# Normalisation units and output projections of an attention layer, kept in two lists instead of one

## The chip, the cores and the metric

The kernel runs on one core of a Trainium2 chip. The metric is the device time of one execution in microseconds, the median of several runs. The profile shows one further execution, with the start and the duration of every instruction on TensorE (PE, and PEld for its weight loads), VectorE (DVE), ScalarE (ACT), GpSimd (POOL) and on SyncE's DMA queue (SP).

## The reference

Four graph layers run one after the other on 2708 nodes with 128 features. Each layer takes a layer norm and a relu of x and adds its result to x. The second is an attention layer, and the change lies there:

```python
def _L1_gnn_ref(x, spatial_encoding, edge_encoding, Wq, Wk, Wv, Wo):
    n, d = x.shape
    h = Wq.shape[0] // d                  # 8
    scale = d ** (-0.5)
    q = (x @ Wq.T).reshape(d, n, h)       # 128 "heads" of 8 columns
    k = (x @ Wk.T).reshape(d, n, h)
    v = (x @ Wv.T).reshape(d, n, h)
    a = jnp.einsum('dnh,dmh->dnm', q, k) * scale
    a = a + spatial_encoding + edge_encoding     # adj, twice
    a = jax.nn.softmax(a, axis=2)
    out = jnp.einsum('dnm,dmh->dnh', a, v)
    out = out.reshape(n, h * d)
    return out @ Wo.T
```

The reshape of `out` matters for the order of the work: a row of the matrix that meets Wo is 1024 neighbouring numbers of the buffer [128 heads, 2708 nodes, 8]. So 128 rows of the output projection need some six heads complete, with all their nodes, and not a slice of every head. Layer 2 (a graph layer that multiplies by the adjacency matrix) needs the layer norm of the rows that come out.

## The kernel before, in words

The 2708 rows lie in 22 tiles of 128 (the last has 20). The 128 heads are worked in 64 pairs (`d`), and two pairs make one of NG = 32 groups of GRP = 4 heads.

*The attention loop.* The softmax over all nodes is taken from a polynomial: moments of keys and values over all nodes, evaluated for every query. The loop runs over the 64 pairs and, in each, over NCH = 6 chunks `c` of the row tiles. One such step issues transposes of the query features (`turn`, L1524, copied out by ACT at L1528), matmuls with the moments (`evaluate`, L1538), a product and a reduction on DVE (L1546, L1555), and parts of the preparation of the next two pairs: query features on DVE and key features on POOL (both by the helper line L802/L805), and the moments (`moments`, L869, weighed on DVE at L883). Every group's sums go to DRAM as `o_g` (`sums`, L1091).

*The work beside the loop.* A step counter `n` counts the 384 steps. A chain of generators, `first`, is advanced by some yields a step; it sorts the nodes, and it computes the exact terms of each node's neighbours, which land in DRAM as `more_n`. When it is exhausted, four calls of `step` follow every step of the loop. `step` advances a generator that is due, or, where none is, lets `begin` start a new one. There are two kinds:

- `normalise(u)`, a unit u. It loads the sums of its heads (L1382 or L1384) and the neighbour terms (L1385), waits LOAD steps, adds them on POOL (L1395), then SOON (one step) later forms the reciprocal (L1400) and the quotients (L1405) on DVE, and then stores the heads to `o_d` with three DMAs (`store_heads`, L551). Units 0 to 14 hold two groups (eight heads), and their sums and terms take two tiles `r_o` and `r_c` of the ring `big` (5 tiles). Units 15 and 16 hold one group, in one tile `r_both`. The last one waits for the end of the loop (HOLD).
- `projected(t)`, a row tile t, by `project_out`. It loads 128 rows of `o_d` (L1034), waits LOAD steps, transposes them with eight matmuls (L1043), lets ACT copy them (L1049), multiplies by Wo (L1061), adds to x on DVE (L1065) and forms the statistics for the layer norm (`measured`, L999). It takes both tiles of one of the rings `c_v` and `c_q`, so that at most two projections are under way. Only one of them may be in its transposes (`turning`) and one in its matmuls (`adding`).

*The order.* Before, one list `beside` holds both kinds in a fixed order, and `begin` only looks at its head. A projection that needs unit `need` stands in it behind unit need + 1, and begins when no unit up to `need` is under way any more, that is, one step after the store was issued. DMAs are issued by SP in their program order: a load that has to wait for the store that it reads holds up those behind it. The two last row tiles (`final`) need the last unit and are projected within layer 2 (L1798).

*After the loop.* Whatever is left of `beside` runs with no attention work between its steps (`while beside or under_way`). Layer norms of groups of four row tiles follow (`normed2`: L1005, L1007, L1008, L1012, and the transposes `turned2`, L1025 and L1026); in the loop they run as soon as four tiles are known. In the last pair, the first four rows of the adjacency matrix for layer 2 are fetched (`rows_of_adj2`, L993), into buffers of the key and query features as these come free. Then comes a branch on `flag`, and the matmuls of layer 2 (L1846).

Of the kernel before, what the change touches and what calls it, by code (L numbers as in the profile page):

```python
# [20 lines left out]
GRP = 4  # L21
# [25 lines left out]
def gnn4_kernel(  # L47
# [28 lines left out]
    NG = C // GRP  # L76
# [129 lines left out]
    with ExitStack() as ph:  # L206
# [56 lines left out]
        with tc.manual_schedule():  # L263
# [37 lines left out]
            for t in begun_with:  # L301
                i = order.index(t)
# [39 lines left out]
            last = iter(())  # L342
            for t0, tw in _cuts(NT, 4):
# [4 lines left out]
                last = now  # L348
# [197 lines left out]
    def store_heads(eng, h0, src):  # L546

        flat = o_d[h0 * N : (h0 + src.shape[1]) * N].rearrange("(i n) k -> i n k", n=N)
        even = WHOLE // 16 * 16
        for p0, p1, nt in ((0, even, NT), (even, WHOLE, NT), (WHOLE, WHOLE + 1, LEFT)):  # L550
            eng.dma_start(  # L551
                flat[:, p0 * NT : p0 * NT + (p1 - p0) * nt].rearrange(
                    "i (p t) k -> p i (t k)", t=nt
                ),
                src[p0:p1, :, :nt].rearrange("p i t k -> p i (t k)"),
            )
# [369 lines left out]
    with ExitStack() as ph:  # L926
# [10 lines left out]
        with tc.manual_schedule():  # L937
# [9 lines left out]
            n = 0  # L947
# [70 lines left out]
    def turned2(t0, t1, pt, copy):  # L1018

        s0 = rows[t0][0]  # L1020
        w = rows[t1 - 1][0] + rows[t1 - 1][1] - s0
        for t in range(t0, t1):
            sz = rows[t][1]
            o = (t - t0) * P
            nc.tensor.transpose(pt[:, o : o + sz], h2[:sz, t], ident[:sz, :sz])  # L1025
        copy(hT2[:, s0 : s0 + w], pt[:, :w])  # L1026
# [41 lines left out]
        measured(t)  # L1068
        known.append(t)

    LOAD, SOON = 4, 1

    with ExitStack() as ph:
        lp = ph.enter_context(tc.tile_pool(name="l1_c", bufs=1, reuse_waits="tile"))
        big = ph.enter_context(tc.tile_pool(name="l1_big", bufs=5, reuse_waits="tile"))
# [283 lines left out]
            yield  # L1361

        def unit_of(g):
            return g // 2 if g < NG - 2 else g - NG // 2 + 1

        NU = unit_of(NG - 1) + 1

        def normalise(u):

            last, two = u == NU - 1, u < NU - 2  # L1370
            nh = GRP * (1 + two)
            h0 = nh * u if two else (NG - NU + u) * GRP
            g = h0 // GRP
            if two:
                ro, co = (
                    big.tile([P, NT * nh * VW], FP, name=f"r_{e}", tag="big") for e in "oc"
                )
            else:
                both = big.tile([P, 2, NT * nh * VW], FP, name="r_both", tag="big")
                ro, co = both[:, 0], both[:, 1]  # L1380
            if two:
                nc.sync.dma_start(ro, o_g[u].rearrange("p j x -> p (j x)"))  # L1382
            elif not last:
                nc.sync.dma_start(ro, o_g[g // 2][:, g % 2])  # L1384
            nc.sync.dma_start(  # L1385
                co.rearrange("p (t x) -> p t x", t=NT),
                more_n[:, h0 : h0 + nh].rearrange("(p t) i k -> p t (i k)", t=NT),
            )
            yield LOAD
            if last:  # L1390
                yield HOLD
            js = 1 + two
            out_ = ro.rearrange("p (j t x) -> p j t x", j=js, t=NT)
            own = ros.pop(g).rearrange("p t i k -> p t (i k)")[:, None] if last else out_
            nc.gpsimd.tensor_tensor(  # L1395
                out_, own, co.rearrange("p (t j x) -> p j t x", j=js, t=NT), ALU.add
            )
            yield SOON
            rs = sm.tile([P, NT * GRP * 2], FP, name="r_rs")[:, : NT * nh]
            nc.vector.reciprocal(rs, ro.rearrange("p (a k) -> p a k", k=VW)[:, :, HEAD])  # L1400
            on = co[:, : nh * NT * HEAD].rearrange("p (i t k) -> p i t k", i=nh, t=NT)
            sums_of = ro.rearrange("p (j t i k) -> p j t i k", j=js, t=NT, k=VW)
            inv = rs.rearrange("p (j t i) -> p j t i", j=js, t=NT)
            for j in range(js):
                nc.vector.tensor_tensor(  # L1405
                    on[:, j * GRP : (j + 1) * GRP].rearrange("p i t k -> p t i k"),
                    sums_of[:, j, :, :, :HEAD],
                    inv[:, j, :, :, None].to_broadcast([P, NT, GRP, HEAD]),
                    ALU.mult,
                )  # L1410
            yield SOON
            store_heads(nc.sync, h0, on)
            yield SOON

        pace = [1.75]

        def faster():

            pace[0] = 4.0
            yield  # L1420

        first = chain(by_node(), sorted_rows(), faster(), from_neighbours())
        beside = []
        done = 0
        late, final = [], []
        for t, (r0, sz) in enumerate(rows):
            need = unit_of(min((((r0 + sz) * P - 1) // N) // GRP, NG - 1))
            while done <= need:
                beside.append((done, done, True))
                done += 1  # L1430
                while late and late[0][1] <= done - 2:
                    beside.append(late.pop(0))
            if need < NU - 1:
                late.append((t, need, False))
            else:
                final.append(t)
        beside += late
        groups = [(t, min(t + 4, final[0])) for t in range(0, final[0], 4)]
        to_turn, norms = [], []
        in_turn = [t for t in range(NT) if t not in final]  # L1440
# [12 lines left out]
        under_way = []  # L1453
        rings = {"big": [], "c_v": [], "c_q": []}
        room = {"big": 5, "c_v": 2, "c_q": 2}
# [8 lines left out]
        def projected(t, ring):  # L1464

            nat, oT = (tm.tile([P, HD], FP, name="o_nat", tag=ring) for _ in range(2))
            both = nat, oT.rearrange("p (k c) -> p k c", k=KC)
            yield from project_out(both, turn_bank, sum_bank, woT, t)

        def begin(summed):  # L1470

            if not beside:
                return None
            i, need, norm = beside[0]
            last = norm and i == NU - 1
            if need >= summed and not last:
                return None
            if not norm and any(e[2] <= need for e in under_way):
                return None
            takes = 1 if norm and i >= NU - 2 else 2  # L1480
            for ring in ("big",) if norm else ("c_v", "c_q"):
                if sum(e[4] for e in rings[ring]) + takes <= room[ring]:
                    beside.pop(0)
                    gen = normalise(i) if norm else projected(i, ring)
                    entry = [gen, None, need if norm else NU, True, takes]
                    rings[ring].append(entry)
                    under_way.append(entry)
                    return entry
            return None

        def step(n, summed):


            entry = next((e for e in under_way if e[1] <= n), None)
            if entry is None:
                entry = begin(summed)
            if entry is None:
                return False
            wait = next(entry[0], None)
            if wait is None:  # L1500
                entry[3] = False
                under_way.remove(entry)
                for ring in rings.values():
                    while ring and not ring[0][3]:
                        ring.pop(0)
            else:
                entry[1] = n + wait
            return True
# [105 lines left out]
        with tc.manual_schedule():  # L1614
            soon, wanted = [], []
            n, owed = 0, 0
# [5 lines left out]
            for d in range(D):  # L1622
                asked, keyed = {}, {}
                for c in range(NCH):
# [36 lines left out]
                    if first is None:  # L1661
                        owed = 0
                        for _ in range(4):
                            step(n, unit_of(max((d - 1) // PG, 0)))
                        if d < D - 1:
                            normalising()
# [4 lines left out]
                g = d // PG  # L1671
# [12 lines left out]
            copies_by = [nc.vector.tensor_copy, nc.scalar.copy]  # L1684
            for e in under_way:
                e[1] = min(e[1], n)
            while beside or under_way:
                if to_turn:
                    turned2(*to_turn.pop(0), ps_g.tile([P, BK], FP, name="g_ps"), copies_by[0])
                    copies_by.reverse()  # L1690
                if not step(n, NU):
                    n += 1
# [8 lines left out]
    with ExitStack() as ph:  # L1701
# [127 lines left out]
        with tc.tile_pool(name="l2_pa", bufs=1, space=PSUM) as pa, tc.manual_schedule():  # L1829
            pgs = [pa.tile([C, BK], FP, name=f"pg{c}") for c in range(NC)]  # L1830
            beside = last_rows()
# [169 lines left out]
    with ExitStack() as ph, tc.manual_schedule():  # L2001
# [15 lines left out]
        def weighed(t):  # L2017
            sz, k = rows[t][1], ROOM[t]
            g = gs[t]
            z = gating(zp, g[:, 1 : k + 1], g[:, 0, C:], sz, k)  # L2020
            yield
            zs[t] = weighing(zp, g[:, 1 : k + 1], z, sz, l_val[:, t, :k], k)
            yield
# [29 lines left out]
        for t in range(NT + 4):  # L2053
# [3 lines left out]
            two = weighed(t - 1) if 0 <= t - 1 < NT else iter(())  # L2057
# [5 lines left out]
    with tc.tile_pool(name="l3_more", bufs=2) as mp, tc.tile_pool(  # L2063
# [3 lines left out]
        last = m1.tile([P, NT], FP, name="last")  # L2067
# [4 lines left out]
        with tc.For_i(0, nc.values_load(ovf, min_val=0, max_val=1)):  # L2072
# [24 lines left out]
            with tc.For_i(0, rounds):  # L2097
                for t, (r0, sz) in enumerate(rows):
# [35 lines left out]
                    g = mp.tile([P, 8, 2 * C], FP, name="g")  # L2134
# [3 lines left out]
                    e = mp.tile([P, C], FP, name="extra")  # L2138
# [48 lines left out]
```

## Time and profile before

| | |
|---|---|
| median of 3 runs | 2151.55 us (2151.46 to 2160.33) |
| the profiled execution | 2157.09 us, its span 2155.3 us |
| mean granted TensorE clock | 0.894 |
| PE busy | 1692.6 us, 79% of the span |
| DVE busy | 1444.2 us, 67% |
| POOL busy | 1321.0 us, 61% |
| ACT busy | 931.8 us, 43% |
| L1395, a unit of eight heads on POOL | 15 times, 3562 ns |
| L1400, its reciprocal on DVE | 15 times, 1246 ns |
| L1405, its quotients on DVE | 30 times, median 916 ns, at most 3191 ns |
| units of four heads | L1395 twice, 1859 and 1856 ns; L1400 twice, 680 ns; L1405 twice, 891 ns |

A row of the profile names the start or the number of instructions, the engine, the line, the operation and the tiles (out<-in). In a timeline the first number is the start from the beginning of the span and the second is the busy time in us; in brackets stands how long the engine had been idle, and what it had been waiting for. A row of waits reads: who waited, for whom, us in all, how often, the longest. A row of windows gives for each stretch its length, then the busy us of each engine with the number of instructions, the granted clock, the DMA share and GB/s.

### The profile page before, as it was taken

The page shows a single profiled execution, that of the slowest core. Times are in us where ns is not written, and L with a number is a line of the kernel's source. Part 1 is how long each engine was busy: PE and PEld are TensorE (multiplying, and loading weights), DVE is VectorE, ACT ScalarE, POOL GpSimd, SP SyncE. Part 2 cuts the span into 40 slices and gives each one's busy share as a digit, 9 for nine tenths or more (in the row PEclk, how much of TensorE's full clock was granted, in tenths as well). Part 3 has the DMA queues.
Part 4 walks back from the last instruction along what each step waited for, and adds up shares of the span by engine and source line. Part 5 has one row for each costly group of instructions (what it writes and reads, how often), then busy time and mean ns, then how long its engine had stood idle before and what let it go on. Part 6 is the DMA issues. An engine that isn't in the chain of part 4 may idle for free. (4 is left out here: it accounts for less than half of the span.)

```text
span 2155.3 us, 30079 instructions
## 1 busy us (share of the span) xinstructions
PE 1692.6 (79%) x10634; PEld 1348.4 (63%) x10634; DVE 1444.2 (67%) x3232; ACT 931.8 (43%) x2049; POOL 1321.0 (61%) x1363
## 2 busy tenths in 40 slices
PE   4767989988889788988888888888889769943442
PEld 3656864488789666666666665667889745423431
DVE  6899846366677788888888888877788720134331
ACT  3947744376677444444444444444445210021010
POOL 1343332066566699999999999997667210057762
PEclk9978999999999999999999999988999979965555
DMA  4755319778799676667766766764767757433331
GB/s 158 298 164 191 134 57 363 294 246 249 240 300 318 177 245 239 225 238 255 252 231 240 237 244 245 250 237 143 228 202 223 242 152 276 155 138 104 94 100 38
DMA packets 256854, 453.68 MB, mean 210 GB/s; under 512 B 112267, under 2 KB 180110, under 8 KB 231483
## 3 DMA queue, kind: packets, MB, share of 16 engines
q1 hardware_dynamic: 225459, 282.79, 39.6%
q0 software_dynamic: 31232, 168.86, 23.0%
q8 instruction: 85, 1.39, 0.3%
q14 instruction: 78, 0.64, 0.1%
HBM read 336.99 MB, written 114.60 MB: 210 GB/s over the span
## 5 line engine op out<-in xcount | busy, mean ns | idle before, releaser
L1538 PE MATMUL g_ps<-mw,fT 128*124 128x124 f32 x2816 | 377.9, 277 | 10.8 <-DVE mw L883 6.2
L869 PE MATMUL m_ps<-y,fk 123*128 123x128 f32 (+1 forms) x2816 | 372.6, 278 | 0.2 <-POOL fk L805 0.2
L1538 PEld LDWEIGHTS g_ps<-mw,fT 128*124 128x124 f32 x2816 | 344.5, 192 | 12.0 <-DVE mw L883 7.1
L869 PEld LDWEIGHTS m_ps<-y,fk 123*128 123x128 f32 (+1 forms) x2816 | 345.6, 194 | 1.3 <-issue 1.0
L1528 ACT COPY fT<-f_ps 128x496 f32<-128x496 f32 (+1 forms) x384 | 208.6, 543 | 242.1 <-PE f_ps L1524 239.9
L1291 PE MATMUL v_ps<-c_v,ident 128*128 128x512 f32 (+1 forms) x484 | 254.3, 651 | 74.7 <-DVE c_v L1274 74.0
L805 POOL TENSOR_TENSOR fk<-kv_t 128x264 f32<-128x264 f32 (+3 forms) x256 | 188.5, 761 | 186.4 <-ACT kv_t L833 185.6
L1546 DVE TENSOR_TENSOR z<-g_ps,bq 124x360 f32<-124x360 f32 (+1 forms) x384 | 191.1, 498 | 163.3 <-PE g_ps L1538 151.0
L1524 PE MATMUL f_ps<-ident,fq 124*128 124x124 f32 x1408 | 222.9, 278 | 94.1 <-DVE fq L802 63.8
L1250 POOL TENSOR_TENSOR c_kv<-c_kv,c_q 128x1024 f32<-128x1024 f32 (+1 forms) x121 | 284.3, 2350 | 5.0 <-DMA c_kv<-kv_n,srt 3.4
L1524 PEld LDWEIGHTS f_ps<-ident,fq 124*128 124x128 f32 x1408 | 167.4, 145 | 188.5 <-issue 90.1
L805 POOL TENSOR_TENSOR y<-kv_t 128x704 f32<-128x704 f32 x128 | 191.0, 1492 | 67.6 <-PE m_ps L869 67.0
L1555 DVE TENSOR_REDUCE o_raw<-z 124x72 f32<-124x360 f32 (+1 forms) x384 | 190.7, 497 | 13.2
L1291 PEld LDWEIGHTS v_ps<-c_v,ident 128*128 128x128 f32 (+1 forms) x484 | 86.8, 200 | 151.7 <-DVE c_v L1274 69.2
L1256 DVE TENSOR_REDUCE c_c<-c_kv 128x128 f32<-128x1024 f32 (+1 forms) x121 | 148.0, 1223 | 50.2 <-POOL c_kv L1250 47.7
L1263 ACT ACTIVATE c_c<-c_c 128x128 f32<-128x128 f32 (+1 forms) x121 | 31.7, 262 | 330.6 <-DVE c_c L1256 312.9
L805 POOL TENSOR_TENSOR fk<-fk,kv_t 128x440 f32<-128x440 f32 (+2 forms) x192 | 154.9, 821 | 5.5 <-ACT fk L772 5.3
L1274 DVE TENSOR_TENSOR c_v<-c_kv,c_c 128x1024 f32<-128x1024 f32 (+1 forms) x121 | 146.6, 1211 | 0.0
L1235 POOL DMA_INDIRECT c_kv<-kv_n,srt x121 | 118.0, 975 | 22.3 <-issue 8.6
L1974 POOL DMA_INDIRECT g<-tab_d,l_nbr x99 | 103.5, 1045 | 30.2 <-issue 29.8
L957 PE MATMUL qkv_ps<-wT,hT 128*128 128x512 f32 (+1 forms) x264 | 116.9, 601 | 0.4 <-ACT hT L438 0.4
L170 POOL TENSOR_TENSOR n_hot<-n_hot,n_fl 128x640 f32<-128x640 f32 (+1 forms) x22 | 34.0, 1545 | 119.6 <-DVE n_hot L164 116.0
(315 smaller groups left out, 2989.0 us busy)
## 6 DMA issues: line engine op xcount, KB each, us to landing
a_nat<-in_adj_dram SPq DMA_DIRECT2D x34, 1354.0 KB
raw<-qkv_d SPq DMA_DIRECT2D x128, 275.0 KB
qkv_d<-qkv SPq DMA_DIRECT2D x21, 1600.0 KB
n_raw<-qkv_d SPq DMA_DIRECT2D x96, 275.0 KB
kv_n<-n_kv SPq DMA_DIRECT2D x16, 1408.0 KB
fk<-in_adj_dram SPq DMA_DIRECT2D x12, 1354.0 KB
o_g<-o_raw SPq DMA_DIRECT2D x31, 396.0 KB
fq<-in_adj_dram SPq DMA_DIRECT2D x9, 1354.0 KB
```

Source lines behind the costliest of these rows:

```text
L805: nc.gpsimd.tensor_tensor(o, x, y, ALU.mult)
L869: nc.tensor.matmul(pms[d][:, :P], fks[d][:sz, t].rearrange("p i f -> p (i f)"), wide[h][:sz, o : o + P], start=t == 0, stop=t == NT - 1,)
L1235: nc.gpsimd.indirect_dma_start(out=kvs[b][:sz, e].rearrange("p c e k -> p (c e k)"), out_offset=None, in_=kv_n.rearrange("n c k -> n (c k) ...
L1250: nc.gpsimd.tensor_tensor(k, k, qs[t][:sz], ALU.mult)
L1256: nc.vector.reduce_sum(cs[b][:sz], kvs[b][:sz, 0, :, 0], axis=AX.X)
L1274: nc.vector.tensor_tensor(z[:sz], kv[:sz, 0, :, 1].rearrange("p (j c) k -> p j c k", j=2), c.rearrange("p (j c) -> p j c", j=2)[:, :, :, None]
L1291: nc.tensor.matmul(accs[t][:sz, j], ident[:sz, :sz], z[:sz, j].rearrange("p c k -> p (c k)"), start=s0 == 0, stop=s0 == ROOM[t] - 1,)
L1524: nc.tensor.transpose(pt[:, m, :USED], fqs[d][:USED, t0 + m].rearrange("p i f -> p (i f)"), ident[:USED, :USED])
L1528: nc.scalar.copy(fts[d, c][:, :n, :USED], pt[:, :n, :USED])
L1538: nc.tensor.matmul(pg[:USED, m, :USED], ft[:, m, :USED], mws[d][:, :USED], start=True, stop=True,)
L1546: nc.vector.tensor_tensor(z[:USED, : 2 * n], pg[:USED, :n] .rearrange("p m (i w) -> p (m i) w", i=2)[:, :, : VW * B_ALL] .rearrange("p a ( ...
L1555: nc.vector.reduce_sum(ros[g][:USED, t0 : t0 + n, i : i + 2].rearrange("p m i k -> p m (i k)"), z[:USED, : 2 * n].rearrange("p (m i) k b - ...
```

## The change

There are now two lists, `to_norm` and `to_project`, and `begin` looks at the heads of both, the units first. A projection begins only when every unit up to the one it needs is `settled`, which it is LAND = 4 steps after its generator ended; `normalise` ends directly after its stores. LOAD is 5 steps instead of 4. Thirteen units of eight heads are left (TWOS = 13), and the last six groups are units of four heads, so there are 19 units instead of 17.

```diff
-    LOAD, SOON = 4, 1
+    LOAD, SOON, LAND = 5, 1, 4
...
         def unit_of(g):
-            return g // 2 if g < NG - 2 else g - NG // 2 + 1
-
-        NU = unit_of(NG - 1) + 1
+            return g // 2 if g < 2 * TWOS else g - TWOS
+
+        TWOS = NG // 2 - 3
+        NU = NG - TWOS
 
         def normalise(u):
 
-            last, two = u == NU - 1, u < NU - 2
+            last, two = u == NU - 1, u < TWOS
             nh = GRP * (1 + two)
-            h0 = nh * u if two else (NG - NU + u) * GRP
+            h0 = nh * u if two else (TWOS + u) * GRP
...
             yield SOON
             store_heads(nc.sync, h0, on)
-            yield SOON
...
-        beside = []
-        done = 0
-        late, final = [], []
+        to_norm, to_project = list(range(NU)), []
+        final = []
         for t, (r0, sz) in enumerate(rows):
             need = unit_of(min((((r0 + sz) * P - 1) // N) // GRP, NG - 1))
-            while done <= need:
-                beside.append((done, done, True))
-                done += 1
-                while late and late[0][1] <= done - 2:
-                    beside.append(late.pop(0))
             if need < NU - 1:
-                late.append((t, need, False))
+                to_project.append((t, need))
             else:
                 final.append(t)
-        beside += late
+        settled = {}
...
-        def begin(summed):
-
-            if not beside:
+        def enter(ring, takes, gen, unit):
+            if sum(e[4] for e in rings[ring]) + takes > room[ring]:
                 return None
-            i, need, norm = beside[0]
-            last = norm and i == NU - 1
-            if need >= summed and not last:
-                return None
-            if not norm and any(e[2] <= need for e in under_way):
-                return None
-            takes = 1 if norm and i >= NU - 2 else 2
-            for ring in ("big",) if norm else ("c_v", "c_q"):
-                if sum(e[4] for e in rings[ring]) + takes <= room[ring]:
-                    beside.pop(0)
-                    gen = normalise(i) if norm else projected(i, ring)
-                    entry = [gen, None, need if norm else NU, True, takes]
-                    rings[ring].append(entry)
-                    under_way.append(entry)
-                    return entry
-            return None
+            entry = [gen, None, unit, True, takes]
+            rings[ring].append(entry)
+            under_way.append(entry)
+            return entry
+
+        def begin(n, summed):
+
+            entry = None
+            if to_norm and (to_norm[0] < summed or to_norm[0] == NU - 1):
+                u = to_norm[0]
+                entry = enter("big", 1 + (u < TWOS), normalise(u), u)
+                if entry is not None:
+                    to_norm.pop(0)
+            if entry is None and to_project:
+                t, need = to_project[0]
+                if all(settled.get(u, n + 1) <= n for u in range(need + 1)):
+                    for ring in ("c_v", "c_q"):
+                        if entry is None:
+                            entry = enter(ring, 2, projected(t, ring), None)
+                    if entry is not None:
+                        to_project.pop(0)
+            return entry
...
             if wait is None:
                 entry[3] = False
                 under_way.remove(entry)
+                if entry[2] is not None:
+                    settled[entry[2]] = n + LAND
...
-            while beside or under_way:
+            while to_norm or to_project or under_way:
```

More of the change, by code (lines that the diff above doesn't have):

```diff
@@ L1495, in step @@
             if entry is None:
-                entry = begin(summed)
+                entry = begin(n, summed)
             if entry is None:
```

## The prediction

> **What bounds the kernel now.** I read the 40 slices first: TensorE runs at eight or nine tenths nearly up to two thirds of the span and then drops. The change touches only the stretch in which normalisations (N) and out-projections (P) run, so I cut that stretch in two: loop beside the attention steps, and tail after the last one.
>
> ```profile
> core 0: us, PE busy (x) PEld busy (x) DVE busy (x) ACT busy (x) POOL busy (x), PEclk, DMA share, GB/s
> 1481.00:1715.00 234.00, 202.53 (x1728) 197.72 (x1726) 191.80 (x419) 103.62 (x241) 144.95 (x110) 0.96 0.74 216
> 1715.00:1765.00 50.00, 23.94 (x115) 20.17 (x112) 14.52 (x35) 9.52 (x21) 7.54 (x9) 0.66 0.64 186
> ```
>
> In the loop no engine is full: PE 87%, DVE 82%. In the tail none is half full, and TensorE's clock is 0.66. Next the waits of the loop:
>
> ```profile
> ACT o_nat L1049 <- PE v_ps L1043: 27.8, 16, 4.1
> ...
> PE f_ps L1524 <- DVE fq L802: 15.7, 9, 6.9
> ...
> PE v_ps L1043 <- DMA o_nat<-o_d: 0.6, 1, 0.6
> ```
>
> A projection's load that reads what was just stored does hold SP (4 to 6 us an issue), but PE waited for it once in the loop, for 0.6 us. What PE waits for is DVE. The timeline shows why:
>
> ```profile
> 1676.09 3.55 POOL L1395 TENSOR_TENSOR r_o<-r_o,r_c 128x1584 f32<-128x1584 f32 x1 [1.07 <-issue]
> 1677.21 5.26 DVE L1405 TENSOR_TENSOR r_c<-r_o,r_rs 128x704 f32<-128x704 f32 x2
> 1682.83 0.44 DVE L1546 TENSOR_TENSOR z<-g_ps,bq 124x270 f32<-124x270 f32 x1
> 1682.86 1.77 PE L1538 MATMUL g_ps<-mw,fT 128*124 128x124 f32 x8 [3.10 <-DVE mw L883]
> 1685.13 1.69 DVE L1405 TENSOR_TENSOR r_c<-r_o,r_rs 128x704 f32<-128x704 f32 x2
> ```
>
> The same two products of a unit took 1.69 us alone and 5.26 us beside the addition of the next unit on POOL; PE stood still behind them.
>
> I then took the start of every L1546, one per attention step, from DVE's timeline. Steps without N or P last 1.36, 2.08, 1.97, 2.0, 2.5 and 3.0 us for c = 0 to 5 (13 us a pair of heads). The 13 steps that carry the reciprocals of units 0 to 13 are together 53.4 us longer than that: 3.8 us a unit of eight heads. The 19 steps that carry only P work are 17.0 us longer together; a least-squares fit over all 75 steps gives 0.8 us for a projection's matmuls and 0.3 for its transposes. One step beside neither lost 3.2 us to L1008, locked behind a POOL addition.
>
> The tail, counted from L = 1715.8 (the last L1555 ends), to the first layer-2 matmul at 1765.2: 49.4 us.
>
> ```profile
> 1711.38 11.57 SPq L1034 DMA_DIRECT2D o_nat<-o_d  x1
> ...
> 1726.59 1.07 PE L1043 MATMUL v_ps<-ident,o_nat 128*128 128x128 f32 x8 [2.60 <-DMA o_nat<-o_d]
> 1727.49 3.58 PE L1061 MATMUL c_c<-woT,o_nat 128*128 128x128 f32 x16
> 1735.24 3.76 PE L1061 MATMUL c_c<-woT,o_nat 128*128 128x128 f32 x16 [4.17 <-DVE x_sb L1065]
> 1741.90 1.94 PE L1043 MATMUL v_ps<-ident,o_nat 128*128 128x128 f32 x8 [2.91 <-DMA o_nat<-o_d]
> 1744.57 3.68 PE L1061 MATMUL c_c<-woT,o_nat 128*128 128x128 f32 x16 [0.73 <-ACT o_nat L1049]
> 1748.09 1.04 PE L1043 MATMUL v_ps<-ident,o_nat 128*128 128x128 f32 x8
> 1749.86 2.05 PE L1061 MATMUL c_c<-woT,o_nat 128*128 128x128 f32 x16 [0.73 <-ACT o_nat L1049]
> 1757.43 1.63 PE L1025 MATMUL g_ps<-ident,n_kv 128*128 128x128 f32 x4 [0.65 <-ACT n_kv L1012]
> 1765.23 1.22 PE L1846 MATMUL pg<-fk,n_kv 128*128 128x512 f32 x1 [6.17 <-DMA o_nat<-o_d]
> ```
>
> It is a chain of latencies: a load 10.8 us late, DVE busy with N units 14 and 15, a load behind their stores, two matmul blocks at half speed, the last layer norms.
>
> **The change, part by part.** From the order in which the two programs issue their work: before, P0 to P15 are finished in the loop and P16 to P19, N14, N15 and N16 fall to the tail. After, only P0 to P11 and the transposes of P12 fit; N0 to N12 (eight heads) and N13 to N16 (four heads) are done in the loop, N17, N18, the matmuls of P12 and all of P13 to P19 in the tail. LAND, the longer LOAD and the strict "all units settled" cost steps, and the projections, now behind the units in line, pay them.
>
> *Units in the loop.* One double less, -3.8 us. Four singles more: POOL 1.86 us against 3.56, reciprocal 0.68 against 1.25 (the rows of r_both and r_o), so about 0.5 of a double, 1.9 us each, +7.6. Net +3.8. Bounds: a single costs at least DVE's own 0.68 + 0.89 (+2.5 net), at most a double's price (+11.4). Bunching can also gain: units 0 and 1, whose additions run in one step, cost 7.75 together, units 2 and 3, a step apart, 10.0 (part of it P); after, 2 and 3, and 4 and 5, run like 0 and 1, worth up to 4.5, so the low end is -2. I take +3.8.
>
> *Projections out of the loop.* Four matmul blocks and three turns fewer: by the fit 4 x 0.8 + 3 x 0.3 = -4.1 us. Bounds: nothing, since the steps with P alone hold 10 blocks and 10 turns after and 11 and 9 before (the four that go had run in DVE's shadow), and PE's full price, 4 x 1.95 + 3 x 1.04 = -10.9. I take -4.1. One early layer norm fewer: the three in the loop cost 3.2 in all, -1.0.
>
> *Waits and queues in the loop.* The LAND gap takes the wait for the store off SP; worth 0.6 us on PE at most, taken as 0. What SP held behind it (raw, r_o, r_c) has a pair of heads of slack; ACT and POOL then waited beside the path. Two more loads of sums and of more_n, and two more sets of three stores, go through SP at 0.4 to 0.6 us an issue; SP's queue has room there. Loop: +3.8 - 4.1 - 1.0 = -1.3.
>
> *Tail.* N17 and N18: POOL adds N18 as soon as the last z is reduced (1.86), DVE does few, flag, a copy and both units, ready at L + 5.2. SP issues their stores, then P14's load, at about L + 7. The adjacency rows hold it no longer: in before 5.4 MB went by from 1708.6 to 1726.6, 300 GB/s; the queue of after has 6.8 MB from the stores of N16 (about L - 19) and 1.4 MB from the last row (free at L - 3), and is empty near L + 8. P14's rows land 3.9 us after the issue, as P18's did (1738.0 to 1741.9): L + 11, as P17's did in before. P12 and P13 are done by L + 6.5 beneath that. Then P14 as P18 (6.2 us from its first transpose to the next projection's), P15 to P19 as P19 (1.04 + 0.73 + 2.05, 3.8 each): L + 36.5. A load follows its own buffer's transposes, so it lands before its turn. Sum and statistics 1.2; layer norms for three groups instead of two (period 2.28, 1757.43 - 1755.16) and three ACT copies: first activation 0.4 later, last one 6.2 after that begins, 1.8 for copies, 46.1. The branch and the fetch of layer 2, 5.5 as before (1759.7 to 1765.2): L + 51.6 against 49.4, so +2.2. N16's 1.5 us on DVE at the end of before is already left out.
>
> *The clock.* The rows: P16, P17 and P18 ran their matmuls at 3.6 to 3.8 us, twice P19's 2.05, all behind idle times of 2.6 to 5 us or in the first microseconds after them. The Trainium skill (TensorE: Matmul & The Clock Gate, "The HAM clock gate") has the clock halved after an idle window of about 3.4 us and full after as long a busy one. By the rule only P14 is cold, its gaps being 0.73 us: the +2.2 above. By the count of rows, three of four cold, some four of P15 to P19 would be, at 6.2 - 3.8 = 2.4 us each, +9.6. The rule speaks against moving PE work from a stretch with clock 0.96 to one with 0.66. As P19 after P18 agrees with it, I stay near it and allow one more cold block: tail +4.6.
>
> Sum: -1.3 + 4.6 = +3.3 us on the profiled execution's 2157.1 (span 2155.3 and 1.8 around it), 2160.4. That execution was 5.5 above the median 2151.55; against the median, 2155.
>
> **The rivals.**
> *The loop was bound by PE after all* (faster). For it: PE 87%. Against it: the fit. Full price -10.9, units at -2, the L1008 stall gone -3.2, tail +2.2: -13.9, 2138.
> *The cold tail* (slower). Between the last g_ps and layer 2, six projections one behind the other instead of two pairs; each waits on PE for ACT (0.73 to 1.1 us), and if the clock stays at half, P15 to P19 take 6.2 us: 5 x 2.4 = 12 on the bare sum, -1.3 + 2.2 + 12 = +13, 2164.5. It passes half a per cent from the fourth cold projection. For it: clock 0.66 in the tail now. Against: P19.
> *Singles cost what doubles cost in the loop*, if each stops DVE for one step whatever its length, and the moved projections had been free: +11.4 + 0 - 1.0 + 4.6 = +15, 2166.5. For it: units of one size cost from 2.35 to 4.66, so position counts for more than length.
> *The stated aim does nothing*: waiting for the store's landing takes away a wait that PE hardly had. This is part of my forecast, not apart from it.
>
> **How the numbers follow.** Half a per cent, 10.8 us, is about what a measurement of this kernel tells from no change. My forecast 48% (own range 2147 to 2163), PE-bound 16%, cold tail 22%, dear singles 14%. Range: 2141 leaves out most of the PE-bound case, 2170 takes in the other two. Faster: 3/4 of the PE-bound case and a little, 0.13. Slower: 3/4 of the cold tail, 4/5 of the dear singles, a bit of the forecast, 0.31. Same 0.56.
>
> **What would show it.** Right: loop from the end of the neighbour stage to the last z within 5 us of 234; L1061 eight projections after L; P14's transposes near L + 11; layer 2 begins at L + 52 to 56. A loop of 222 us or less says PE-bound; 3.7 us blocks on P15 to P19 say cold; a loop over 240 says dear singles. P14 landing after L + 16 would mean that I misjudged the adjacency loads.

## The result, and the profile after

The changed kernel is slower: 2176.17 us median of 4 runs (2175.64 to 2180.14) against 2154.41 us (2151.46 to 2160.33, four runs), ratio 1.0102, 95% interval 1.0074 to 1.0129. That is above the predicted range (2141 to 2170) and above the half per cent taken as no change. The profiled execution took 2175.64 us, its span is 2173.8 us against 2155.3. Chips differ in their absolute times (the kernel before took 2142 to 2158 us in the experiments), so experiments are compared by their ratio to the kernel before on their own chip.

Layer 2 begins at 1787.85 us instead of 1765.23, 22.6 us later; what follows it is 4.1 us shorter (385.9 against 390.1), which I have not explained; the code there is the same in both. In the profiled executions of the experiments that part took 372 to 378 us, and 389 on the one chip where the kernel before took 2158, so the differences between chips seem to lie there and not in the stretch compared here.

To divide the 22.6 alike for every kernel, "loop" is from here on the time between the first DVE products z of steps 309 and 384, and "tail" the time from the latter to the first matmul of layer 2. The loop took 255.1 us after and 233.8 before (+21.2 unrounded), the tail 52.9 and 50.3 (+2.6); the loop began 1.2 us earlier. Loop and tail are read from one profiled execution of each kernel, whose time lay up to 9.4 us from the median of its runs (a_apart), so differences of a few us between kernels mean nothing; the ratios come from all runs. The windows of the changed kernel, cut where its loop and tail end:

```profile
core 0: us, PE busy (x) PEld busy (x) DVE busy (x) ACT busy (x) POOL busy (x), PEclk, DMA share, GB/s
1480.00:1735.00 255.00, 198.70 (x1634) 194.01 (x1633) 199.05 (x411) 98.75 (x230) 153.18 (x114) 0.89 0.75 213
1735.00:1788.00 53.00, 31.33 (x207) 26.95 (x207) 14.04 (x44) 15.54 (x34) 2.22 (x7) 0.80 0.31 105
```

The loop is 21 us longer with 3.8 us less of PE work and 7.3 us more of DVE's. PE's share fell from 87% to 78% and its clock from 0.96 to 0.89, while the tail's clock rose from 0.66 to 0.80: the reverse of what the cold-tail rival feared. Who waits, in the same loop (us in all, times, longest):

```profile
PE f_ps L1525 <- DVE fq L802: 38.3, 10, 10.4
ACT o_nat L1049 <- PE v_ps L1043: 30.9, 11, 7.0
PE g_ps L1539 <- DVE mw L883: 7.0, 1, 7.0
PE v_ps L1043 <- DMA o_nat<-o_d: 5.6, 1, 5.6
```

The first row was 15.7 us in nine waits of at most 6.9. (`fq` holds the query features, `f_ps` their transposes.) PE's transposes now wait 38.3 us for query features that DVE has not yet made. The timeline shows what DVE did meanwhile, here with units 0 and 1 (start, us, engine, line):

```profile
1491.23 7.08 POOL L1396 TENSOR_TENSOR r_o<-r_o,r_c 128x1584 f32<-128x1584 f32 x2
1492.85 0.44 DVE L1547 TENSOR_TENSOR z<-g_ps,bq 124x270 f32<-124x270 f32 x1
1494.83 1.25 DVE L1401 RECIPROCAL r_rs<-r_o 128x176 f32<-128x176 f32 x1 [0.28 <-POOL r_o L1396]
1496.12 5.00 DVE L1406 TENSOR_TENSOR r_c<-r_o,r_rs 128x704 f32<-128x704 f32 x2
1498.28 2.10 POOL L805 TENSOR_TENSOR fk<-kv_t 128x704 f32<-128x704 f32 x1
1500.34 1.70 POOL L805 TENSOR_TENSOR fk<-fk,kv_t 128x440 f32<-128x440 f32 x1
1501.05 1.24 DVE L1401 RECIPROCAL r_rs<-r_o 128x176 f32<-128x176 f32 x1
1502.32 3.26 DVE L1406 TENSOR_TENSOR r_c<-r_o,r_rs 128x704 f32<-128x704 f32 x2
1503.42 2.58 POOL L805 TENSOR_TENSOR fk<-fk,kv_t 128x264 f32<-128x264 f32 x2
1505.51 0.52 DVE L1547 TENSOR_TENSOR z<-g_ps,bq 124x360 f32<-124x360 f32 x1
1508.87 1.06 PE L1525 MATMUL f_ps<-ident,fq 124*128 124x124 f32 x4 [10.44 <-DVE fq L802]
```

Both additions run back to back on POOL. Once the first is done, both reciprocals and all four quotients (two rows of two) follow one another on DVE: 10.7 us, from 1494.83 to 1505.51, in which DVE does nothing for the attention loop. PE stands still for 10.44 us, and its first four transposes afterwards take 1.06 us, where four of them in a loop that had not stalled took 0.59 in the kernel before. Units 0 and 1 were such a pair before, too, and six more units stood only a step apart; what is new is that twelve of the thirteen units of eight heads now come two by two. Where in the six steps of a pair of heads the units fall matters as well: units 0 and 1 lengthened their step by 7.75 us before and by 10.7 after, where they come one step later. No experiment varied that alone.

The tail, PE's timeline:

```profile
1747.77 1.94 PE L1043 MATMUL v_ps<-ident,o_nat 128*128 128x128 f32 x8 [5.12 <-DMA o_nat<-o_d]
1750.44 3.78 PE L1061 MATMUL c_c<-woT,o_nat 128*128 128x128 f32 x16 [0.73 <-ACT o_nat L1049]
1754.01 1.91 PE L1043 MATMUL v_ps<-ident,o_nat 128*128 128x128 f32 x8
1756.66 2.05 PE L1061 MATMUL c_c<-woT,o_nat 128*128 128x128 f32 x16 [0.73 <-ACT o_nat L1049]
...
1771.28 2.05 PE L1061 MATMUL c_c<-woT,o_nat 128*128 128x128 f32 x16 [0.73 <-ACT o_nat L1049]
...
1787.85 2.92 PE L1847 MATMUL pg<-fk,n_kv 128*128 128x512 f32 x3 [5.52 <-DMA o_nat<-o_d]
```

Only P14's block of 16 matmuls ran at half speed (3.78 us); every later one took 2.05. The transposes of P14 and of P15 were slow too (1.94 and 1.91 us, against 1.04 for those of P16 to P19).

### The profile page after: what moved, and what is told of

Its sections match the earlier page's. It is cut to its first block, busy times and chain, and to the rows that moved or that the text cites. A ratio compares the mean times of both kernels' runs of the same rounds, so it can differ in the third digit from the quotient of the medians.

```text
span 2173.8 us, 30120 instructions
## 1 busy us (share of the span) xinstructions
PE 1697.2 (78%) x10634; PEld 1350.8 (62%) x10634; DVE 1452.2 (67%) x3233; ACT 932.6 (43%) x2050; POOL 1325.9 (61%) x1365
## 3 DMA queue, kind: packets, MB, share of 16 engines
q0 software_dynamic: 31232, 168.86, 22.5%
## 5 line engine op out<-in xcount | busy, mean ns | idle before, releaser
L1539 PE MATMUL g_ps<-mw,fT 128*124 128x124 f32 x2816 | 383.6, 279 | 9.2 <-DVE mw L883 7.6
L1539 PEld LDWEIGHTS g_ps<-mw,fT 128*124 128x124 f32 x2816 | 350.6, 195 | 10.2 <-DVE mw L883 8.3
L805 POOL TENSOR_TENSOR fk<-kv_t 128x264 f32<-128x264 f32 (+3 forms) x256 | 190.4, 769 | 192.2 <-ACT kv_t L833 191.2
L805 POOL TENSOR_TENSOR y<-kv_t 128x704 f32<-128x704 f32 x128 | 190.9, 1492 | 71.0 <-PE m_ps L869 70.4
L1556 DVE TENSOR_REDUCE o_raw<-z 124x72 f32<-124x360 f32 (+1 forms) x384 | 190.8, 497 | 13.2
L1256 DVE TENSOR_REDUCE c_c<-c_kv 128x128 f32<-128x1024 f32 (+1 forms) x121 | 148.1, 1224 | 52.2 <-POOL c_kv L1250 49.7
L805 POOL TENSOR_TENSOR fk<-fk,kv_t 128x440 f32<-128x440 f32 (+2 forms) x192 | 155.7, 826 | 14.8 <-ACT fk L772 14.6
```

The lines of the kernel that those rows point to most:

```text
L805: nc.gpsimd.tensor_tensor(o, x, y, ALU.mult)
L1256: nc.vector.reduce_sum(cs[b][:sz], kvs[b][:sz, 0, :, 0], axis=AX.X)
L1539: nc.tensor.matmul(pg[:USED, m, :USED], ft[:, m, :USED], mws[d][:, :USED], start=True, stop=True,)
L1556: nc.vector.reduce_sum(ros[g][:USED, t0 : t0 + n, i : i + 2].rearrange("p m i k -> p m (i k)"), z[:USED, : 2 * n].rearrange("p (m i) k b - ...
```

## The experiments

My theory after the result: DVE takes two units in one unbroken stretch, because the units now stand first in a list of their own and the ring has room for two of them; what stands queued behind them on DVE is late, and PE with it. The rivals: the projections' longer waits (LOAD and LAND), the size of the units, and the lock that keeps DVE and POOL apart. I use the measure "stalls" for PE's idle times of over 1 us in the loop, added up: 25.6 us before, 53.6 after. A "stretch" is the time from a unit's instruction on DVE to the next one of the loop there, with nothing but units' instructions (and waits for them) between.

**a_apart.** The changed kernel, but a unit begins at the earliest three steps after the last one began.

```diff
+        apart = [0]
...
-            if to_norm and (to_norm[0] < summed or to_norm[0] == NU - 1):
+            if n >= apart[0] and to_norm and (to_norm[0] < summed or to_norm[0] == NU - 1):
...
                     to_norm.pop(0)
+                    apart[0] = n + 3
```

> After, but a unit may begin no sooner than three steps behind the one before it. Pairs theory (the loop grew because units of eight heads now come two by two, so that VectorE works through two of them in one or two steps, one of them locked behind GpSimd's addition, and TensorE cools down): the twelve doubles in pairs cost 4.6 us each now and should cost the 3.35 of those that came alone in before, and the slow steps behind the long stops go, so 15 to 20 us come off the loop: 2156 to 2161. Waits theory (LOAD, LAND and the later projections cost it): no change, 2176. Size theory (units of four heads are dear): no change.

Measured: 0.9995 (0.9984 to 1.0007) of the kernel before; loop 229.1 us, tail 51.6, stalls 28.6, longest stretch 6.5 us instead of 10.7. The whole loss is gone by spacing alone, and more than the 15 to 20 us that I expected. In the groups of the loop (busy us and mean ns, then PE's idle time before it by releaser) the changed kernel and this one stand like this:

```profile
L1525 PE MATMUL f_ps<-ident,fq 124*128 124x124 f32 x271 | 46.1, 293 | 40.2 <-DVE fq L802 38.3 <-ACT fT L1529 1.6
```

```profile
L1528 PE MATMUL f_ps<-ident,fq 124*128 124x124 f32 x271 | 44.7, 286 | 19.4 <-DVE fq L802 17.9 <-ACT fT L1532 1.3
```

The same 271 matmuls, and 20.4 us less of waiting for fq. The units' products took 40.9 us for the 30 in the loop, against 45.6 for the same 30, so shorter products are 4.7 of the 26 us.

**a_land.** The changed kernel with the waits of before.

```diff
-    LOAD, SOON, LAND = 5, 1, 4
+    LOAD, SOON, LAND = 4, 1, 1
```

> After with LOAD back at 4 and LAND at 1 instead of 4, so that 16 instead of 12 projections fit in the loop. Waits theory: most of the loss comes back, 2155 to 2160. Pairs theory: the loop keeps its pairs of units and gets four projections more, 255 to 260 us; the tail loses four at 3.8 us each; 2163 to 2168.

Measured: 1.0072 (1.0047 to 1.0097); loop 264.2, tail 34.1, stalls 49.7. Shorter waits bring four projections back into the loop: the tail falls by 19 us and the loop grows by 9. PE waited in the loop 13.2 us for the loads of o_nat instead of 5.6, so LAND and LOAD do keep a wait away that the new order would have. Whether that costs more than it saves is not settled by this pair, whose intervals overlap (a_apart_land below settles it). Most of the loss is still there.

**a_two15** and **a_two0.** The changed kernel with 15 units of eight heads and two of four, as before, and with units of four heads only.

```diff
-        TWOS = NG // 2 - 3
+        TWOS = NG // 2 - 1     # a_two15
+        TWOS = 0               # a_two0
```

> After with units of four heads for the last two groups only, as before, and eight heads for the rest. Size theory: most of the loss comes back. Pairs theory: two more doubles in a pair instead of four singles, 0 to 5 us slower than after, 2176 to 2181.

> After with units of four heads for all groups. In after three singles that came alone cost their steps 1.4, 2.0 and 0.5 us, 1.3 each. Pairs theory: stops of VectorE are half as long and the lock half as long, 28 singles at 1.5 to 2 us are 42 to 56 against 66 us in the loop: 2156 to 2166. Size theory: 2185 or more, from the four-head units' many short DMA rows (twice as many descriptors in all) and twice as many issues.

Measured: a_two15 1.0087 (1.0062 to 1.0113), loop 253.3, tail 52.2, stalls 50.2. Its interval overlaps that of the changed kernel, so whether units of four heads for the last groups cost or gain is not settled; the loss is there without them. a_two0: 1.0045 (1.0027 to 1.0062), loop 245.1, tail 47.5, stalls 39.2. With small units alone the loss is about halved. That two small units in a row make a shorter stretch than two large ones would explain it, but was not shown: the longest stretch here is 9.1 us.

**b_pair** and **b_apart.** The kernel before, with its units made to go two by two, and with them spaced as in a_apart.

```diff
             takes = 1 if norm and i >= NU - 2 else 2
+            if norm and i % 2 == 0 and i < NU - 3 and any(e[3] for e in rings["big"]):
+                return None
...
-                while late and late[0][1] <= done - 2:
+                while done % 2 == 0 and late and late[0][1] <= done - 2:
```

```diff
-        def begin(summed):
+        apart = [0]
+
+        def begin(n, summed):
...
+            if norm and n < apart[0]:
+                return None
...
                     beside.pop(0)
+                    if norm:
+                        apart[0] = n + 3
```

> Before, with nothing changed but that units begin two together: an even unit waits until no unit is left in the ring. LOAD 4, no LAND, the old order and unit sizes stay. Pairs theory: seven pairs at the 8 to 10.7 us that pairs cost in after, instead of 53 us in all: 60 to 70, so the loop grows by 8 to 17 us with nothing else of the change: ratio to before 1.003 to 1.008. Its rival now, that it is the later start of each unit against the projections that counts (units first in line), says no change, 1.000.

> Before, with units at least three steps apart. Four of its units pairs go; pairs theory: 8 doubles fall from 4.15 to 3 us or less, ratio 0.995 or a little below if the tail stays. Rival: 1.000.

Measured: b_pair 1.0054 (1.0035 to 1.0072), loop 249.4, tail 45.0, stalls 35.2: pairs, in the old list with the old waits, lengthen the loop by 15.6 us and give 5.3 back in the tail. The edit also moves the projections behind a pair, so it is not pairs and nothing else: 15 of them instead of 16 are multiplied in the loop. Its lateness shows in another row, too: PE waited 9.1 us for fq, but 17.5 us for L1065, a projection's addition on DVE, in four waits. b_apart 0.9966 (0.9955 to 0.9976), loop 225.5, tail 49.6, stalls 19.6: even the few pairs of the kernel before cost it a third of a per cent.

**a_split.** The changed kernel, pairs and all, with a step between the reciprocal and each product.

```diff
             for j in range(js):
+                yield SOON
```

> After, with a step between the reciprocal of a unit and each of its products, so units still come in pairs but VectorE's stretch in one step is a third as long. If the length of VectorE's stretch starves TensorE (transposes wait for query features), the stalls over 5 us go and 10 us or more come off after's loop of 255 us. If it is the lock against GpSimd's additions, the products are as long as in after (44 us) and the loop stays over 250.

Measured: 0.9998 (0.9987 to 1.0008), loop 231.6, tail 51.2, stalls 24.7; PE's wait for fq falls to 21.1 us, with one wait of 7.2 left. The units still begin two by two, but no unit puts two of its instructions in a row on DVE any more; the two units of a pair still do, one each, and the longest stretch is 6.5 us. It repairs what a_apart repairs, so a pair is not dear as such. The products fell too, however, below the 41.3 us of the changed kernel (shown under a_dveadd):

```profile
L1407 DVE TENSOR_TENSOR r_c<-r_o,r_rs 128x704 f32<-128x704 f32 x26 | 32.5, 1278 | 0.0
```

So this run alone does not tell the stretch from the lock; a_all, below, tells more.

**a_apart_land.** Spacing, and the waits of before.

> After with units three steps apart, LOAD 4 and LAND 1. From the runs so far: the loop of a_apart, 229 us, plus the 9 us that a_land's loop has over that of after, and the tail of a_land, 34: 272 against 284 of before, so 12 us faster than before, ratio 0.994. If what a_apart saved hangs on LAND's gap, the loop is 250 or more and the ratio 1.000.

Measured: 0.9949 (0.9930 to 0.9967), loop 243.5, tail 33.5, stalls 27.9. Without pairs, the shorter waits (LOAD and LAND together) are worth 0.5% beside a_apart, and the intervals do not touch: a tail 18 us shorter and a loop 14 us longer.

**a_dveadd.** The changed kernel with the units' addition on DVE, so that it and the products can't lock each other out. (POOL's key features, L805, still can.)

```diff
-nc.gpsimd.tensor_tensor(out_, own, ...
+nc.vector.tensor_tensor(out_, own, ...
```

> After, with a unit's addition on VectorE instead of GpSimd. It takes the lock between the two away (products back near 0.9 us each, 26 us instead of 44 in the loop) and makes VectorE's stretch of a pair longer by two additions[...]. If the lock is what made pairs dear, the loop loses 10 us or more (245 or less). If it is the length of the stretch, the gain of 18 us in the products and the cost of some 25 us in additions leave the loop at 255 to 265.

Measured: 1.0143 (1.0120 to 1.0166), loop 263.5, tail 52.4, stalls 60.3. The groups of DVE in a_dveadd, and then the products of the changed kernel:

```profile
L1406 DVE TENSOR_TENSOR r_c<-r_o,r_rs 128x704 f32<-128x704 f32 x26 | 28.1, 1119 | 0.4
L1396 DVE TENSOR_TENSOR r_o<-r_o,r_c 128x1584 f32<-128x1584 f32 x13 | 28.0, 2165 | 0.4 <-DMA r_c<-more_n 0.4
```

```profile
L1406 DVE TENSOR_TENSOR r_c<-r_o,r_rs 128x704 f32<-128x704 f32 x26 | 41.3, 1628 | 0.4
```

The products are 13.2 us shorter together, but DVE has 28.0 us of additions more, and the loop is longer by 8.4. The additions come a step ahead of the reciprocals, not in one stretch with them. The first pair, with the row of PE after it:

```profile
1494.02 5.66 DVE L1396 TENSOR_TENSOR r_o<-r_o,r_c 128x1584 f32<-128x1584 f32 x2
1501.20 1.25 DVE L1401 RECIPROCAL r_rs<-r_o 128x176 f32<-128x176 f32 x1
1502.48 2.94 DVE L1406 TENSOR_TENSOR r_c<-r_o,r_rs 128x704 f32<-128x704 f32 x2
1505.34 1.24 DVE L1401 RECIPROCAL r_rs<-r_o 128x176 f32<-128x176 f32 x1
1506.62 1.69 DVE L1406 TENSOR_TENSOR r_c<-r_o,r_rs 128x704 f32<-128x704 f32 x2
1511.60 1.06 PE L1525 MATMUL f_ps<-ident,fq 124*128 124x124 f32 x4 [9.27 <-DVE fq L802]
```

Between 1499.6 and 1501.2 DVE does 1.6 us of the loop's work, and PE still stands for 9.27 us. No stretch of this run is over 7.2 us, so the longest stretch alone does not measure the loss: two stretches with so little between them act nearly as one.

**a_all.** The changed kernel with spacing, splitting and the waits of before together.

> After with units three steps apart, a step between reciprocal and products, LOAD 4 and LAND 1. a_apart_land had a loop of 243.5 and a tail of 33.5. If splitting still shortens what is left of the stretches, 5 us come off: loop 238, ratio to before 0.992. If spacing has already taken all there was, 0.995.

Measured: 0.9891 (0.9868 to 0.9914), 2121.16 us against 2143.34 on that chip; loop 214.5, tail 47.5, stalls 12.3. It is the fastest of all, a per cent below the kernel before. I had expected a loop of 238 and a ratio of 0.992; the loop came out 24 us shorter than that and the tail longer than the 33.5 of a_apart_land, with 14 projections multiplied in the loop instead of 15, and why splitting gained so much here was not taken apart. In its groups:

```profile
L1407 DVE TENSOR_TENSOR r_c<-r_o,r_rs 128x704 f32<-128x704 f32 x26 | 39.2, 1507 | 0.0
```

```profile
L1529 PE MATMUL f_ps<-ident,fq 124*128 124x124 f32 x277 | 44.0, 278 | 13.4 <-DVE fq L802 12.9
```

The products are nearly as long as in the changed kernel (1507 ns against 1628), and all 30 in the loop take nearly as much (43.9 us against 45.6), yet its loop is 40 us shorter. DVE's timeline of a_all shows where they went:

```profile
1506.77 1.24 DVE L1401 RECIPROCAL r_rs<-r_o 128x176 f32<-128x176 f32 x1
...
1508.32 0.44 DVE L1551 TENSOR_TENSOR z<-g_ps,bq 124x270 f32<-124x270 f32 x1
...
1509.14 0.88 DVE L1407 TENSOR_TENSOR r_c<-r_o,r_rs 128x704 f32<-128x704 f32 x1
1510.51 0.53 DVE L1551 TENSOR_TENSOR z<-g_ps,bq 124x360 f32<-124x360 f32 x1 [0.49 <-PE g_ps L1543]
...
1511.52 1.07 DVE L1407 TENSOR_TENSOR r_c<-r_o,r_rs 128x704 f32<-128x704 f32 x1
```

Reciprocal and products are parted by the loop's own z; in this unit DVE is away from the loop for 1.2, 0.9 and 1.1 us, instead of 10.7 at a time. The longest stretch in the whole loop is 4.1 us.

**b_apart_split.** Spacing and splitting in the kernel before.

> Before with units three steps apart and a step between reciprocal and products. b_apart had a loop of 225.5 and a tail of 49.6 with ratio 0.9966. Splitting takes 3 to 6 us more off the loop but moves one or two projections to the tail, since each unit takes two steps more: ratio 0.994 to 0.998.

Measured: 1.0048 (1.0035 to 1.0062), loop 225.6, tail 73.2, stalls 22.5. That is a miss: the loop is no shorter than b_apart's, though two projections and a unit fewer are done in it, and the tail is 24 us longer. In one list a unit that takes more steps holds up the projections and units behind it, and more of both falls to the tail, where PE's timeline has waits such as these:

```profile
1713.97 1.94 PE L1043 MATMUL v_ps<-ident,o_nat 128*128 128x128 f32 x8 [10.54 <-DMA o_nat<-o_d]
...
1739.89 3.75 PE L1061 MATMUL c_c<-woT,o_nat 128*128 128x128 f32 x16 [4.64 <-DVE x_sb L1065]
```

Splitting therefore pays with the two lists (a_split, a_all), and not in this form with the one.

**a_all15.** a_all with 15 units of eight heads.

> The fastest so far (units three steps apart, reciprocal and products in steps of their own, LOAD 4, LAND 1; ratio 0.9891) with units of four heads for the last two groups only. If units of four heads pay once units no longer bunch, it is slower, 0.992 or more; if they matter as little as in the run that gave after 15 doubles, it lies at 0.988 to 0.991.

Measured: 0.9919 (0.9895 to 0.9943), loop 223.3, tail 48.3, stalls 14.6. The intervals overlap: units of four heads for the last groups may gain a quarter of a per cent here, or nothing.

| kernel | ratio to before | loop us | tail us | stalls us | longest stretch us |
|---|---|---|---|---|---|
| before | 1 | 233.8 | 50.3 | 25.6 | 7.9 |
| after | 1.0102 | 255.1 | 52.9 | 53.6 | 10.7 |
| a_apart | 0.9995 | 229.1 | 51.6 | 28.6 | 6.5 |
| a_split | 0.9998 | 231.6 | 51.2 | 24.7 | 6.5 |
| a_land | 1.0072 | 264.2 | 34.1 | 49.7 | 10.9 |
| a_apart_land | 0.9949 | 243.5 | 33.5 | 27.9 | 7.4 |
| a_two15 | 1.0087 | 253.3 | 52.2 | 50.2 | 10.7 |
| a_two0 | 1.0045 | 245.1 | 47.5 | 39.2 | 9.1 |
| a_dveadd | 1.0143 | 263.5 | 52.4 | 60.3 | 7.2 |
| a_all | 0.9891 | 214.5 | 47.5 | 12.3 | 4.1 |
| a_all15 | 0.9919 | 223.3 | 48.3 | 14.6 | 4.0 |
| b_pair | 1.0054 | 249.4 | 45.0 | 35.2 | 9.9 |
| b_apart | 0.9966 | 225.5 | 49.6 | 19.6 | 5.5 |
| b_apart_split | 1.0048 | 225.6 | 73.2 | 22.5 | 3.9 |

## Why the prediction was wrong

*Tail: right.* P14's transposes began 11.9 us after the last reduction of the loop ended (L = 1735.9; predicted 11), P19's matmuls ended at L + 37.4 (predicted 36.5), and layer 2 began at L + 51.9: near the bare 51.6, without the further cold block that I had allowed. Part of that closeness is luck: up to P19 it ran 0.9 us late, behind it 0.6 early. The load past the adjacency rows was issued at about L + 8.1 and its rows were used 3.8 us later, close to the steps of the forecast (7 and 3.9).

*Clock: the rule held for the matmuls, and in part for the rest.* The granted clock was at half from 1746.37 to 1756.61, that is from 3.7 us after P13's matmuls ended to just behind P15's transposes. P14, behind 5.12 us of idle, took 3.78 us for its matmuls; the blocks behind gaps of 0.73 us took 2.05. The Trainium skill's rule (TensorE: Matmul & The Clock Gate, "The HAM clock gate") agrees with every block of matmuls here, and counting slow rows would have been wrong. The clock came back only 8.8 us after P14 began, though, later than the busy window of some 3.4 us that the rule asks for; the pauses of 0.7 us in between may have kept it down, which no run here shows. That made P15's transposes slow (1.91 us against 1.04), which my sum had left out. The cold-tail rival fell. The clock falls in the loop instead, which I did not ask for: behind the stall of 10.44 us it was at half for 5.4 us of work, and after the long stalls eight steps ran 0.8 to 1.1 us over their usual time.

*Loop: wrong*, -1.3 forecast and +21.2 measured. By the same sum over steps:

| us over the bare steps | before | after | change | predicted |
|---|---|---|---|---|
| steps that carry units | 53.4 | 66.2 | +12.7 | +3.8 |
| steps with projections alone | 17.0 | 21.6 | +4.6 | -4.1 |
| other | 4.9 | 8.7 | +3.8 | -1.0 |

The step that failed is "Units in the loop". Its counts were right, and so was the price of a unit of four heads: the three in the loop that run alone cost 1.4, 2.0 and 0.5 us, on average 1.3, below the 1.9 that I took and far from a double's price, so the dear singles did not happen, though a loop over 240 us was my sign for them. What failed is one price for a double, 3.8, with "bunching can also gain" as its low end. In the changed kernel units 0 to 11 come in six pairs and cost 55.5 us, 4.6 each (10.7 together for the first pair; one pair's 11.0 holds the 5.6 us wait for a load). The units that stood alone before cost 3.35 on average. I had read the one pair of before (units 0 and 1, 7.75 us together) against the next two units (10.0 us), and took the difference for a gain of pairing, though those two came only a step apart and were dear themselves. Against the mean of the units that stood alone it was a loss of 1 us. b_pair and a_apart show the sign and the size: pairing costs some 15.6 us of loop in the old kernel, and spacing returns 26 in the new one. With its units spaced the rest of my sum held: by the same count a_apart's loop differs from before's by +0.8 us in the steps with units (forecast +3.8) and by -5.5 in all others (forecast -5.1).

*Projections.* The predicted -4.1 does not show: four blocks and three turns fewer, and their steps cost 4.6 us more. (How the last two rows divide depends on where a step that fits both is put; together they cost 8.4 us more.) Some of these steps follow a stall and run slowly, and one projection's matmuls share a step with a pair; how much each adds was not separated. In a_apart, with the same twelve projections in its loop as in the changed kernel, the steps without units are 14 us shorter than there, so this cost, too, hangs on the pairs.

*Waits of SP, the stated aim.* I had put it at nothing. In the changed order the wait would exist (13.2 us in a_land against 5.6), and avoiding it by LAND and LOAD moves four projections to the tail. Net the longer waits lose 0.3% with bunched units, where the intervals overlap, and 0.5% with spaced ones, where they do not.

*Early layer norm.* The stall of 3.2 us at L1008 is gone, as forecast; the other steps swallowed it.

*The PE-bound rival* fell with the loop: 3.8 us less PE work and a longer loop. The fault that decided was one that neither forecast nor rivals held: I followed the order of the instructions, but asked of each what it costs, and not how long the run of them is on DVE before the loop gets its turn. My reading of the rows held only in part, too: I put the 5.26 us of two products down to the addition beside them. Rows like them in the changed kernel show POOL's key features holding products up as well (last section).

## What to carry to other kernels

Work put beside a loop on an engine that the loop needs is to be priced by how long it keeps the engine from the loop at a time, and not only by its sum: 45.6 us of products, in stretches of up to 10.7 us, made this loop 23 to 26 us longer than 41 or 37 us of them spaced (a_apart) or parted by the loop's own work (a_split), and with 43.9 us in stretches of at most 4.1 us the loop was the shortest of all (a_all). Stretches with only a little of the loop's work between them count together (a_dveadd). How far ahead the loop's producers run should set what length is harmless; that was not varied here. When a new rule lets a kind of side work start as soon as it can, look in the new order for items that now stand back to back, and space or split them. A single row that is better than its dear neighbours is no proof of a gain; compare it with all of its kind.

## What the runs showed of the hardware

A DVE product with both inputs in SBUF is held up while POOL works, and not by the additions alone. Two products took 1.69 us alone. In the first pair of the changed kernel the first product took 2.94 us and ended 0.75 us after the addition that ran beside it. The other three had no addition beside them, but POOL's key features (L805), and took 2.14, 1.89 and 1.45 us. Of the 26 such products in the loop, 17 overlap the key features only and take 1.55 us on average, five overlap an addition and take 2.49, four overlap neither and take 0.89. DVE's z, with an operand in PSUM (0.44 us), and the reciprocal with one input (1.25) ran inside the same 7.08 us of additions unhindered. The Trainium skill (SBUF — State Buffer, "SBUF: two separate sides") tells of a lock on a port pair that only some of DVE's forms need, and these rows agree. What I had not expected is that the lock is no measure of the loss. With the additions off POOL the products took 1119 ns each on average instead of 1628, and the kernel was slower (1.0143), though that run has 28.0 us of additions more on DVE; and the fastest kernel had the lock nearly in full (1507 ns a product).

The addition of 128x1584 numbers took 1.8 to 3.1 us on DVE, at the median 1.9 (in a_dveadd), and 3.5 us on POOL (7.08 for two). The mean of 2165 ns on DVE is no plain speed: the slowest took 3.07 us, with POOL at work beside it.
